# Stacks of split queries and keys through a DRAM copy, six transfers per projection, and new priorities for the order of the work

## The chip, the cores and the metric

The kernel runs on one core of a Trainium2 chip. A core has TensorE (PE, matrix products; its weight loads are shown as PEld), VectorE (DVE), ScalarE (ACT), GpSimd (POOL) and SyncE (SP, whose queue issues most DMA transfers). Each runs its own list of instructions in order and waits on semaphores for the others. The metric is the time of one execution on the device in microseconds, as the median of several runs.

## The reference

The input is `x`, 16 graphs of 1024 nodes with 256 features, and one adjacency matrix of 1024 x 1024. Four layers follow each other, each `x = x + layer(relu(layernorm(x)))`. The first three are graph attention; in short, with `H` = 4, 1 and 1 heads:

```python
q = h @ W                                   # (B, N, H*D)
e = leaky_relu(e_src[:, :, None] + e_dst[:, None, :])
attn = softmax(where(adj > 0, e, -big), over neighbours)
out = elu(attn @ q)                         # relu in the second layer
```

The fourth is a transformer block with eight heads of 32 features:

```python
q, k, v = split(h @ w_qkv)
scores = einsum('fnhd,fmhd->fhnm', q, k) / sqrt(32)
t = softmax(where(adj > 0, scores, -1e9)) @ v
y = layernorm(h + t)
out = layernorm(y + relu(y @ w1 + b1) @ w2 + b2)
```

All is float32.

## The kernel before

Everything of interest is in `direct` (a second path, `general`, runs only if a check of number ranges fails, and does not run here). A graph has eight tiles of 128 nodes (`NT = 8`), two halves of 512 nodes (`HALF`), and two groups of four heads in the fourth layer (`CT = 2`, `HG = 4`).

**Recording and planning.** No function issues instructions at once. `pe`, `act`, `dve`, `pool` and `dma` append a piece of work to a record, with its planned duration and the buffers that it writes and reads. After all 16 graphs are recorded, `schedule` (L189) orders every engine's list: it walks through a planned time, and on each engine takes, of the work that is ready, that of the lowest key. The key comes from `priority` (L136): the number of the graph plus a value on a line through knots (`KNOTS`, L283), one set for each stage (`gat0` to `gat2` for the graph attention layers, `values` and `steps` for the fourth layer's attention, `feed` for its feed-forward part, `last` for that of the last graph, `beside` for the second graph's first layer), with a shift per engine (`LEAD`). So work of several graphs is interleaved, and the knots decide how. `PASS` (L117) is the planned time in which a result reaches another engine, `SWITCH` and `BIAS` are the planned cost of TensorE's mode changes, `SLACK` and `AHEAD` belong to the model of transfers (L260 to L263). The planned times only set the order; on the chip, semaphores decide when an instruction starts.

**The graph attention layers** (`gat`, L725). Transposes (L529), projection (L770), a row of exponentials that goes to DRAM and comes back on all partitions (L843, L852), weights on VectorE (L868), then products: L895 for one head, and for four heads L982 and L992, which use the matrix engine as four column tiles of 32.

**The fourth layer's attention** (`attention`, L1082). For each group and half, `project` (L1125) makes queries or keys: a product (L1132), a copy rounded to float32r on ScalarE called `hi` (L1141), and the rest `lo = x - hi` on VectorE (L1144). There is one `hi` and one `lo` buffer. A score then is one float32r product over 128 rows in which each head's 32 features stand four times (hi.hi, hi.lo, lo.hi, lo.lo), so each head's rows of `hi` and `lo` have to be moved to a stack, `qs` for queries and `ks` for keys: 4 blocks of 32 partitions, with the four heads side by side. Sixteen transfers from on-chip memory to on-chip memory on SyncE's queue do this (L1154), each 32 partitions of 2 KB, 64 KB in all. Eight projections are made for each graph; `later` sets before which step the last five are recorded.

Then come 32 steps per graph (group, half, tile of keys): scores (L1352), exponentials on ScalarE (L1376), mask on VectorE (L1385), two steps later the product with the values and with ones (L1217, column tiles again). Some of the sums over tiles are made on VectorE (L1244) and by accumulating transfers from GpSimd's queue (L1253). At the end of each half are copies (L1292), transposes and the division. `feed` follows (L1449 and around), with the input brought back from DRAM (L1502) and the result stored (L1574). `x` is loaded at L1597 and put into DRAM at L1634.

On-chip rings set how far work can run ahead: four matrix result banks `sc` for scores and projections, four `bank`, six buffers `pa`, one `ks`, two `qs`.

Of the kernel before, what the change touches and what calls it, by code (L numbers as in the profile page):

```python
# [113 lines left out]


WEIGHT = {"pe": 1.0, "dve": 0.3}
PASS = {"pe": 0.198, "act": 0.153, "dve": 0.202, "pool": 0.13, "dma": 0.0}  # L117


class Work:  # L120


    def __init__(self, engine, us, emit, key, modes, moved, lands):
        self.engine, self.us, self.emit, self.key, self.modes = engine, us, emit, key, modes
        self.pass_on = PASS[engine]
        self.moved = moved
# [9 lines left out]
def priority(x):  # L136
    base, knots, total, lead = x.stream
    at = x.pos / max(total, 1e-9) * (len(knots) - 1)
    k = max(0, min(int(at), len(knots) - 2))
    key = base + knots[k] + (knots[k + 1] - knots[k]) * (at - k)  # L140
    return round(key - (LEAD.get(x.engine, 0.0) if lead else 0.0), 6)


class Record:
# [44 lines left out]
    def schedule(self):  # L189
        for n, x in enumerate(self.work):  # L190
            x.n = n
            if x.key is None:
                x.key = priority(x)
            x.left = len(x.before)
            for y in x.before:
                y.after.append(x)
        free = dict.fromkeys(PASS, 0.0)
        queue = 0.0
        future = {e: [] for e in PASS}
        now = {e: [] for e in PASS}  # L200
        mode = "full"
        for x in self.work:
            if not x.left:
                heapq.heappush(future[x.engine], (x.ready, x.n, x))

        def opening(x):

            at, need = 0.0, {}
            for buf in x.opens:
                need[buf.ring] = need.get(buf.ring, 0) + 1  # L210
            for ring, n in need.items():
                if len(ring.free) < n:
                    return None
                at = max(at, sorted(ring.free)[n - 1][0])
            return at

        def turn(x):

            return BIAS * SWITCH.get((mode, x.modes[0]), 0.0) if x.engine == "pe" else 0.0

        def choose(e):

            at = free[e]
            while future[e] and future[e][0][0] <= at:
                x = heapq.heappop(future[e])[2]
                heapq.heappush(now[e], (x.key, x.n, x))
            best = None
            for key, n, x in now[e]:
                t = opening(x)
                if t is not None:  # L230
                    best = min(best or (1e9,), (max(at, t), key + turn(x), n, x))
            if future[e] and (best is None or future[e][0][0] < best[0]):
                for t, n, x in sorted(future[e]):
                    if opening(x) is not None:
                        t = max(t, at, opening(x))
                        best = min(best or (1e9,), (t, x.key + turn(x), n, x))
                        break
            return best

        order = []  # L240
        while True:
            choices = [(c, e) for c, e in ((choose(e), e) for e in PASS) if c]
            if not choices:
                break
            (at, _, n, x), e = min(choices, key=lambda c: c[0][0])
            if (x.key, n, x) in now[e]:
                now[e].remove((x.key, n, x))
                heapq.heapify(now[e])
            else:
                future[e].remove((x.ready, n, x))  # L250
                heapq.heapify(future[e])
            for buf in x.opens:
                _, k = heapq.heappop(buf.ring.free)
                buf.k, buf.t = k, buf.ring.tiles[k]
            us = x.us
            if e == "pe":
                us += SWITCH.get((mode, x.modes[0]), 0.0)
                mode = x.modes[1]
            x.start = at
            if x.moved:  # L260
                queue = max(at + (us if e == "pool" else 0.2), queue) + x.moved
                us = max(us, queue - at - AHEAD)
                x.pass_on = queue + x.lands + SLACK - (at + us)  # L263
            order.append(x)
            free[e] = at + us
            for buf in x.shared:
                buf.end = max(buf.end, at + us + x.pass_on)
                buf.uses.remove(x)
                if not buf.uses:
                    heapq.heappush(buf.ring.free, (buf.end, buf.k))  # L270
            for y in x.after:
                y.ready = max(y.ready, at + us + (x.pass_on if y.before[x] else 0.0))
                y.left -= 1
                if not y.left:
                    heapq.heappush(future[y.engine], (y.ready, y.n, y))
        assert len(order) == len(self.work)
        self.end = max(free.values())
        return order


AHEAD = 3.5
SLACK = 0.56
KNOTS = {  # L283
    "gat0": (-6.706, -3.534, -2.307, -1.522, -2.815),
    "gat1": (0.005, 0.503, 0.618, 0.731, 0.916),
    "gat2": (0.938, 0.468, 0.637, 0.867, 1.15),
    "beside": (0.241, 1.203, 1.943, 0.54, 4.121),
    "values": (1.06, -3.362, -0.305, 3.145, 0.767),
    "steps": (1.014, 1.448, 1.59, 2.064, 1.794),
    "feed": (2.016, 2.165, 2.509, 2.154, 2.609),  # L290
    "last": (2.808, 3.335, 3.547, 5.206, 6.138),
}
BIAS = 1.225
LEAD = {"act": 9.55, "dve": -0.732}

SWITCH = {
    ("full", "col4"): 0.137,
# [7 lines left out]
def act_us(n, pointers=0, sbuf=0):  # L305
    return (n / 1.2 + 41 + 50 * sbuf + 101 * pointers) / 1000
# [14 lines left out]
def mm_us(n):  # L321
    return 2 * max(2 * n / 2.4 + 3.0, 109) / 1000
# [5 lines left out]
def direct(ctx, tc, flag, x, adj, gat_w, gat_a, w_qkv, ln1_g, ln1_b, ln2_g, ln2_b, w1, b1, w2, b2, out):  # L328


    nc = tc.nc
# [3 lines left out]
    HALF = N // 2  # L335
    TH = NT // 2
    D3 = C // H3
    HG = P // D3
# [31 lines left out]
    def ring(name, n, shape, pool=work):  # L370
        return Ring([pool.tile([P] + shape, F32, name=f"{name}{i}") for i in range(n)])
# [32 lines left out]
    dram = ctx.enter_context(tc.tile_pool(name="dram", bufs=1, space=DRAM))  # L404
    r_x3 = ring("x3", 3, [NT, C], dram)
    r_rd = ring("rd", 4, [P], dram)
    r_rt = ring("rt", 1, [P])
    r_sc = ring("sc", 4, [HALF], psum)
    r_bank = Shared([psum.tile([P, HALF], F32, name=f"bank{i}") for i in range(4)])
# [8 lines left out]
    def pe(us, emit, w, r, modes=("full", "full")):  # L418
        rec.add("pe", us, emit, w, r, modes)

    def act(us, emit, w, r):
        rec.add("act", us, emit, w, r)
# [7 lines left out]
    def dma(moved, lands, emit, w, r, key=None, us=0.57, engine="dma"):  # L430
        rec.add(engine, us, emit, w, r, key=key, moved=moved, lands=lands)
# [650 lines left out]
    def attention(b, xt, b_mv, b_rstd):  # L1082
# [42 lines left out]
        def project(g, hf, keys, stack, at):  # L1125

            sc, hi, lo = r_sc.new(), r_hi.new(), r_lo.new()
            c0 = keys * C + g * P

            def product():  # L1130
                for ct in range(CT):
                    nc.tensor.matmul(  # L1132
                        sc.t,
                        wqkv_sb[:, ct, c0 : c0 + P],
                        hT.t[:, ct, hf * HALF : (hf + 1) * HALF],
                        start=ct == 0,
                        stop=ct == CT - 1,
                    )

            pe(CT * mm_us(HALF), product, [sc], [b_qkv] + [hT((ct, hf)) for ct in range(CT)])  # L1140
            act(act_us(HALF), lambda: nc.scalar.copy(hi.t.bitcast(F32R), sc.t), [hi], [sc])  # L1141
            dve(
                tt_us(HALF),
                lambda: nc.vector.tensor_sub(lo.t, sc.t, hi.t),  # L1144
                [lo],
                [sc, hi],
            )
            for a in range(4):
                part = ((hi, hi, lo, lo), (hi, lo, hi, lo))[keys][a]
                for r in range(HG):  # L1150
                    dma(
                        0.3,
                        1.5,
                        lambda: nc.sync.dma_start(  # L1154
                            stack.t[a * D3 : (a + 1) * D3, r, at : at + HALF],
                            part.t[r * D3 : (r + 1) * D3, :],
                        ),
                        [stack((r, hf if keys else 0, a))],
                        [part],
                        us=0.59,  # L1160
                    )

        def values(it):
            sc = r_sc.new()
# [47 lines left out]
        steps = [(g, hf, jt) for g in range(CT) for hf in range(2) for jt in range(NT)]  # L1212
# [19 lines left out]
        for n in range(len(steps) + LAG):  # L1232
            m = n - LAG
            if m >= 0:
                g, hf, jt = steps[m]
# [12 lines left out]
                elif jt % run:  # L1248
                    for ss, pt in zip(sums[g, hf], pas[m]):
# [6 lines left out]
                            us=1.135,  # L1256
# [81 lines left out]
            if n < len(steps):  # L1338
                g, hf, jt = steps[n]
# [928 lines left out]
```

## Time and profile before

| what | value |
|---|---|
| median of 3 runs | 4092.49 us (4090.72 to 4097.2) |
| the profiled execution's own time | 4091.28 us |
| its span, first to last instruction | 4089.5 us |
| mean granted TensorE clock | 0.995 |
| busy: PE, PEld, DVE, ACT, POOL | 98%, 58%, 86%, 66%, 16% |
| mean DMA rate | 95 GB/s |
| SyncE's queue / GpSimd's queue | 22.4% / 16.2% of the 16 DMA engines' time |
| L1154, stack transfers | 2048, median 0.588 us of SyncE each |

The profile is one execution. Busy time of an engine is the union of its instructions' spans. Matmuls are pipelined and overlap, so that a busy PE is not PE at its peak. A line number is that of the kernel's source; a name such as `qs<-lo` says which tile is written from which.

### The profile page before, as it was taken

To read this page: it belongs to the slowest core of one execution; us is meant where nothing else is said; L and a number is where in the kernel's file an instruction comes from. 1 tells how busy PE (TensorE), PEld (TensorE's weight loads), DVE (VectorE), ACT (ScalarE), POOL (GpSimd) and SP (SyncE) were. 2 spreads that over 40 slices of the span, in tenths; PEclk is the share of its full clock that TensorE was granted. 3 is DMA by queue.
4 is the path that set the end of the run, shared out by engine and by line. 5 is a ranking of instruction groups with operands and counts; after the bars stand their busy time and mean duration, and the time that the engine had idled before them with its cause. 6 is when DMAs were issued, how large, how long until landed. Compare 5 with 4: busy or idle time off the path is not lost.

```text
span 4089.5 us, 68377 instructions
## 1 busy us (share of the span) xinstructions
PE 4023.3 (98%) x23874; PEld 2354.7 (58%) x23874; DVE 3499.0 (86%) x5994; ACT 2689.9 (66%) x6673; POOL 646.7 (16%) x631
## 2 busy tenths in 40 slices
PE   7999999999999999999999999999999999999998
PEld 3566466564655646566564665646556465665643
DVE  7768898988979799897988989889797998979866
ACT  5467676775757767576675767757577675765765
POOL 1102011121211202111121211212111011111100
PEclk9999999999999999999999999999999999999999
DMA  3024344343444324443243443434443244432441
GB/s 128 24 77 102 99 109 99 89 93 98 101 112 102 90 75 112 114 108 90 77 105 99 109 105 87 95 92 103 110 109 85 74 112 113 108 90 59 107 103 47
DMA packets 215248, 389.65 MB, mean 95 GB/s; under 512 B 45168, under 2 KB 80240, under 8 KB 214896
## 3 DMA queue, kind: packets, MB, share of 16 engines
q1 hardware_dynamic: 180336, 259.36, 22.4%
q0 software_dynamic: 34560, 125.84, 16.2%
q8 instruction: 191, 3.13, 0.3%
q14 instruction: 161, 1.32, 0.1%
HBM read 91.03 MB, written 33.95 MB: 31 GB/s over the span
## 4 chain that ended last, share of the span: by engine, by line
PE 85%; DVE 5%; ACT 4%; SPq 2%; DMA 2%; issue 1%; POOL 1%; DVEq 0%; ACTq 0%; POOLq 0%
PE bank L895 20%; PE bank L1217 14%; PE sc L1352 11%; PE bank L982 9%; PE bank L770 9%; PE bank L529 6%; PE bank L992 5%; PE bank L1449 4%; PE sc L1132 4%; PE sc L1169 2%; SPq L1154 2%; DVE pt L868 2%; DVE pa L1385 1%; POOL rstdz L466 1%; ACT waste L446 1%
## 5 line engine op out<-in xcount | busy, mean ns | idle before, releaser
L1385 DVE TENSOR_TENSOR pa<-pa,mask 128x1024 f32<-128x1024 f32 x1024 | 1221.4, 1218 | 72.4 <-ACT pa L1376 69.4
L1376 ACT ACTIVATE pa<-sc 128x512 f32<-128x512 f32 x2048 | 1098.3, 606 | 234.2 <-PE sc L1352 175.1
L868 DVE SCALAR_TENSOR_TENSOR pt<-row,e,mask 128x512 f32<-128x512 f32 x1472 | 1016.3, 744 | 62.2 <-DMA row<-rd 40.3
L895 PE MATMUL bank<-qb,pt 128*128 128x257 f32 x4096 | 942.0, 380 | 3.5 <-ACT fz L1533 3.5
L895 PEld LDWEIGHTS bank<-qb,pt 128*128 128x128 f32 x4096 | 771.3, 189 | 147.1 <-ACT pa L1376 12.6
L1352 PE MATMUL sc<-qs,ks 128*128 128x512 f32 x2048 | 717.7, 455 | 11.2 <-DMA qs<-lo 5.8
L1217 PE MATMUL bank<-pa,va 128*32 128x512 f32 x4096 | 504.8, 596 | 0.3 <-DVE pa L1385 0.2
L1352 PEld LDWEIGHTS sc<-qs,ks 128*128 128x128 f32 x2048 | 360.4, 189 | 212.3 <-ACT pa L1376 56.5
L1244 DVE TENSOR_TENSOR sums<-pa,pa 128x1024 f32<-128x1024 f32 x360 | 430.3, 1219 | 57.6 <-PE bank L1217 57.4
L982 PE MATMUL bank<-pt,qb 128*32 128x512 f32 x3840 | 468.7, 597 | 2.4 <-DVE pt L868 1.4
L770 PE MATMUL bank<-w_aug,hT 128*128 128x259 f32 (+1 forms) x1504 | 383.1, 393 | 0.5 <-ACT hT L764 0.5
L1253 POOL DMA_DIRECT2D sums<-pa x240 | 210.1, 878 | 930.5 <-DVE pa L1385 507.2
L770 PEld LDWEIGHTS bank<-w_aug,hT 128*128 128x128 f32 x1504 | 275.8, 191 | 121.1 <-ACT pa L1376 13.7
L923 ACT ACTIVATE ex<-bank,rec 128x256 f32<-128x256 f32 x256 | 122.1, 477 | 294.5 <-DVE rec L915 287.6
L982 PEld LDWEIGHTS bank<-pt,qb 128*32 128x32 f32 x3840 | 118.8, 109 | 275.9 <-issue 193.0
L1217 PEld LDWEIGHTS bank<-pa,va 128*32 128x32 f32 x4096 | 120.5, 109 | 263.0 <-issue 227.6
L992 PE MATMUL bank<-pt,e 128*32 128x512 f32 x1920 | 258.5, 592 | 0.0
L500 ACT ACTIVATE hn<-xh,mv,rstd 128x256 f32<-128x256 f32 x376 | 195.9, 592 | 93.0 <-DVE mv L490 89.1
L1132 PE MATMUL sc<-hTa,wqkv_sb 128*128 128x512 f32 x512 | 244.4, 600 | 0.1
L466 POOL TENSOR_TENSOR rstd<-rstd,neg_half 128x4 f32<-128x4 f32 x96 | 138.5, 1443 | 597.0 <-DVE rstd L458 588.3
L820 POOL TENSOR_TENSOR sum_e<-sum_e,e 128x12 f32<-128x12 f32 (+1 forms) x94 | 114.7, 1220 | 648.2 <-ACT e L781 648.1
L1141 ACT CAST hi<-sc 128x512 fp32r<-128x512 f32 x128 | 74.8, 585 | 196.4 <-PE sc L1132 72.8
(152 smaller groups left out, 4638.4 us busy)
## 6 DMA issues: line engine op xcount, KB each, us to landing
sums<-pa POOLq DMA_DIRECT2D x240, 512.0 KB, 6.0
row<-rd SPq DMA_DIRECT2D x184, 256.0 KB
ks<-hi SPq DMA_DIRECT2D x512, 64.0 KB
ks<-lo SPq DMA_DIRECT2D x512, 64.0 KB
qs<-hi SPq DMA_DIRECT2D x512, 64.0 KB
qs<-lo SPq DMA_DIRECT2D x512, 64.0 KB
xh<-in_x_dram SPq DMA_DIRECT2D x32, 512.0 KB
x<-xh SPq DMA_DIRECT2D x32, 512.0 KB
```

The lines of the kernel that those rows point to most:

```text
L529: nc.tensor.transpose(dst(k), src(k), ident[:shape, :shape])
L770: nc.tensor.matmul(g.t[:, : C + 3 * H], hT.t[:, ct, k * P : (k + 1) * P], w_aug[l][:, ct, :], start=ct == 0, stop=ct == CT - 1,)
L868: lambda: nc.vector.scalar_tensor_tensor(pt.t, row.t, e3[:, 2, jt // TH, h, jt % TH : jt % TH + 1], mask[:, jt, hf * HALF : (hf + 1) * HAL ...
L895: nc.tensor.matmul(g.t[:, : D + 1], pts[jt].t[:, k * P : (k + 1) * P], qb[:, jt, 0, :], start=jt == 0, stop=jt == NT - 1,)
L982: nc.tensor.matmul(g.t[u * D + d : u * D + d + D3, :], qb[:, j, h + u, d : d + D3], pts[u][j - jt].t, start=j == 0, stop=j == NT - 1,)
L992: nc.tensor.matmul(gd.t[c : c + D3, :], one(jt + k, h + u).to_broadcast([P, D3]), pts[u][k].t, start=jt == 0, stop=jt == NT - 2,)
L1132: nc.tensor.matmul(sc.t, wqkv_sb[:, ct, c0 : c0 + P], hT.t[:, ct, hf * HALF : (hf + 1) * HALF], start=ct == 0, stop=ct == CT - 1,)
L1217: nc.tensor.matmul(ac.t[r * D3 : (r + 1) * D3, :], columns(r), of_head(r), start=first, stop=last,)
L1244: lambda: nc.vector.tensor_add(ss.t, p0.t, p1.t),
L1352: nc.tensor.matmul(scs[r - r0].t, ks.t[:, r, jt * P : (jt + 1) * P].bitcast(F32R), q.t[:, r, :].bitcast(F32R), start=True, stop=True,)
L1376: lambda: nc.scalar.activation(pt.t[:, v, :], sc.t, AF.Exp, scale=1.0 / math.sqrt(D3)),
L1385: lambda: nc.vector.tensor_mul(pt.t, pt.t, mask[:, jt : jt + 1, i0 : i0 + HALF].to_broadcast([P, 2, HALF]),),
```

## The change

Two things are changed. First, `project` writes `hi` and `lo` (256 KB each) into a buffer in DRAM, of which there are three, and fills each of the stack's four blocks with one transfer from there; that takes all four heads at once, 128 rows of 2 KB. That makes two transfers to DRAM and four back, in place of sixteen. Second, the planner's constants and the knots are other ones; most stages have nine knots in place of five, and the model of a transfer that finds the queue full is a fixed duration in place of one that grows.

```diff
-PASS = {"pe": 0.198, "act": 0.153, "dve": 0.202, "pool": 0.13, "dma": 0.0}
+PASS = {"pe": 0.122, "act": 0.556, "dve": 0.232, "pool": 0.13, "dma": 0.0}
...
             if x.moved:
+                if e == "dma" and queue - at > BEHIND:
+                    us = max(us, HELD)
                 queue = max(at + (us if e == "pool" else 0.2), queue) + x.moved
-                us = max(us, queue - at - AHEAD)
                 x.pass_on = queue + x.lands + SLACK - (at + us)
...
-AHEAD = 3.5
-SLACK = 0.56
+BEHIND, HELD = 2.0, 1.35
+SLACK = 0.722
 KNOTS = {
-    "gat0": (-6.706, -3.534, -2.307, -1.522, -2.815),
+    "gat0": (-10.926, -10.742, -7.218, -4.626, -2.628, -2.099, -0.444, -3.636, -2.816),
...
-    "steps": (1.014, 1.448, 1.59, 2.064, 1.794),
-    "feed": (2.016, 2.165, 2.509, 2.154, 2.609),
+    "steps": (0.98, 1.188, 1.323, 1.512, 1.578, 1.712, 2.006, 2.02, 1.489),
+    "feed": (2.026, 2.163, 1.768, 1.658, 2.343, 1.828, 2.009, 2.223, 3.042),
...
 }
-BIAS = 1.225
-LEAD = {"act": 9.55, "dve": -0.732}
+BIAS = 2.241
+LEAD = {"act": 8.212, "dve": 0.635}
...
+    r_hl = ring("hl", 3, [2, HALF], dram)
...
+            hl = r_hl.new()
+            for k, part in enumerate((hi, lo)):
+                dma(0.65, 1.5, lambda: nc.sync.dma_start(hl.t[:, k, :], part.t), [hl(k)], [part])
             for a in range(4):
-                part = ((hi, hi, lo, lo), (hi, lo, hi, lo))[keys][a]
-                for r in range(HG):
-                    dma(
-                        0.3,
-                        1.5,
-                        lambda: nc.sync.dma_start(
-                            stack.t[a * D3 : (a + 1) * D3, r, at : at + HALF],
-                            part.t[r * D3 : (r + 1) * D3, :],
-                        ),
-                        [stack((r, hf if keys else 0, a))],
-                        [part],
-                        us=0.59,
-                    )
+                k = ((0, 0, 1, 1), (0, 1, 0, 1))[keys][a]
+                dma(
+                    1.0,
+                    1.83,
+                    lambda: nc.sync.dma_start(
+                        stack.t[a * D3 : (a + 1) * D3, :, at : at + HALF],
+                        hl.t[:, k, :].rearrange("(r d) n -> d r n", r=HG),
+                    ),
+                    [stack((r, hf if keys else 0, a)) for r in range(HG)],
+                    [hl(k)],
+                )
```

## The prediction

> **What bounds the kernel now.** I read the page's busy table first, then the busy time by stages, then the chain of waits in order of time at the end of the span, then TensorE's own waits there.
>
> ```profile
> span 4089.5 us, 68377 instructions
> PE 4023.3 (98%) x23874; PEld 2354.7 (58%) x23874; DVE 3499.0 (86%) x5994; ACT 2689.9 (66%) x6673; POOL 646.7 (16%) x631
> ```
>
> ```profile
> 0.00:250.00 250.00, 221.53 (x1413) 131.23 (x1414) 179.28 (x399) 129.50 (x359) 28.63 (x34) 0.97 0.23 75
> 1000.00:1250.00 250.00, 249.44 (x1502) 146.27 (x1498) 220.46 (x376) 169.04 (x426) 44.00 (x40) 1.00 0.40 98
> 3750.00:4000.00 250.00, 240.35 (x1271) 139.95 (x1270) 190.60 (x295) 167.61 (x396) 32.88 (x35) 0.99 0.42 99
> 4000.00:4090.00 90.00, 73.00 (x407) 30.43 (x405) 57.37 (x94) 51.08 (x118) 5.79 (x7) 0.92 0.15 40
> ```
>
> The stage lines give PE, PEld, DVE, ACT, POOL, granted clock, DMA share. In the middle PE is busy 249.4 of 250 us, VectorE 220, ScalarE 169: the matrix engine is the bound, and a few us per batch is all that waiting can cost. Start and end are looser.
>
> Busy PE is not dense PE, so I priced the matmuls by the distance between starts in the trace where they follow each other closely.
>
> ```profile
> 144.50 13.98 PE bank L895 x64
> ...
> 3939.25 3.57 PE bank L1217 x32
> 3949.25 5.29 PE bank L1217 x48
> ```
>
> 64 records of L895 in 13.98 us are 0.216 each plus the last one's tail. Thirty-two column-tiled records take 3.57 us and 48 take 5.29: 16 more cost 1.72, so four cost 0.43, and 3.57 - 8 x 0.43 = 0.13 is what leaving that mode costs. Entering it costs 0.094 (0.309 to the next start after a 0.215 us matmul). Over all kinds: 4096 x 0.216 (L895) + 11936/4 x 0.429 (L982, L992, L1217) + 2048 x 0.231 (L1352) + 1536 x about 0.220 (L770) + 1024 x 0.429 (L1132, L1449) + 512 x 0.216 (L1169) + about 2720 transposes x 0.109 = 3825 us dense. There are 397 column-tiled stretches x 0.23 = 92 us of mode changes. The span's other 173 us are 22 us before the first and after the last matmul, and 151 us in which a matmul came late. By stage, from the same starts: 44 us of lateness in the first 300 us, 38 us after 3700 us, and about 4.8 us in each batch between (period 247.6 us; dense work and mode changes 242.8).
>
> The end shows where the stack transfers matter:
>
> ```profile
> PE sc L1352 <- DMA qs<-lo: 5.8, 1, 5.8
> ```
>
> ```profile
> 3912.86 0.59 SPq L1154
> 3913.50 1.22 SPq L1154
> ...
> 3915.40 2.03 DMA ks<-lo
> ...
> 3923.99 1.97 DMA qs<-lo
> ...
> 3926.10 1.41 PE sc L1352 x2
> ```
>
> The last batch has nothing beside it, and its first scores wait 5.8 us for the stack. SyncE issues one small transfer per 0.63 us; two stacks are 32 issues, from 3903.5 to 3923.99, and the last lands 1.97 us later. This is the only long TensorE wait on a DMA; in the middle no matmul waits for one.
>
> **What the Trainium skill says.** "TensorEngine Tiling (Array Packing)", Key Properties: a change of tiling mode drains the array. The trace agrees: 0.13 + 0.094 us per stretch. "DMA: Bandwidth & Descriptors", Rules for kernel authors: coalesce, since under 64 KB a transfer is mostly overhead, and a DMA that reads what another wrote must wait for its semaphore. The trace agrees on the first (64 KB: 0.59 us issue, 2.0 us to land); no run here yet shows the second. "TensorE: Matmul & The Clock Gate", Part 1: after about 3.4 us without matmuls the clock halves. The trace agrees: half clock for 6.8 us from 3925.0, just after that 5.8 us wait, and for 3.4 us from 248.8.
>
> **The change, part by part.** The built programs hold the same instructions on PE, VectorE and ScalarE; only order and transfers differ.
>
> *Transfers.* 128 projections x 16 = 2048 issues of 0.63 us (81 us of SyncE per batch) become 128 x 6 = 768. The write to DRAM is 256 KB; the nearest row is the store of the result, issue 0.40, landing 2.15. The read is 256 KB; the nearest is the reload of x, issue 0.33, landing up to 3.14:
>
> ```profile
> 4069.63 2.15 DMA out_dram<-xr
> 4071.80 3.14 DMA xr<-x
> ```
>
> The destination's 32 partitions might keep the issue at 0.59; I take 0.33 to 0.63. One projection then needs, from hi's copy: 0.5 (copy) + 0.7 (lo on VectorE) + 0.4 + 2.15 (write) + 2 x 0.6 + 2.0 to 3.1 = 7 to 8 us; before 0.5 + 16 x 0.63 + 2.0 = 12.6. It adds a wait: the reads stand on SyncE's in-order queue until their write has landed, up to 2.2 us each time, and behind them stand row spreads for VectorE, reloads of x and stores. In the middle this is free: in the new order the shortest PE work between a projection and the first scores that use its stack is 23.4 us (before 18.4), three times the need. That is its cover; without it each us of lateness on all eight stacks costs 8 us per batch, over 100 us in the kernel. Hi and lo (one buffer each) come free after one landing instead of eight issues; ScalarE waited 47.7 us and VectorE 28.7 us on these in the whole kernel, both off the bound.
>
> At the end: in the new order two projections' transfers interleave. From hi: 0.5 + 12 issues x 0.33 to 0.63 (4 to 7.6) + two landings of 2.15 that the queue can't fill + 2.0 to 3.1 = 11 to 15.5 us, against 12.3 us of PE work between the second projection and its first scores (before 16.8 and 5.8 late). So it is 0 to 3 us late; I take 1. Gain 5 us, and with under 3.4 us of silence the half-clock stretch goes (6.8 x 1/2 = 3.4): 8 us. At the start the same two projections stand, with half clock once (1.7 us) and several waits of 1.3 to 2.9 us from 244 to 290 us; I take a gain of 6 (bounds 0 and 12).
>
> *Order.* Counted in the order: 413 column-tiled stretches, 24 per batch instead of 23: 16 x 0.23 = +3.7 us. Then, for each matmul that waits for a ScalarE or VectorE instruction which itself waits for a matmul, I took the dense PE work between those two matmuls, less the awaited instruction's duration in its row and 0.45 us for both hand-overs. Between the first batch's end and the last's start, 185 of 2346 such margins were under 0.6 us and 30 under zero; in the new order 28 of 2394 and 14. With up to fifteen instructions queued ahead on that engine counted as well, those under 0.6 us go from 643 to 287. The 4.8 us of lateness in one batch: seven gaps of 0.12 to 0.5 us make 2.1, ends of L1352 and transposes; the rest are gaps of some 0.05 us after nearly every change of kind. I take 1.8 of the 2.1 as gone and the rest as staying: (1.8 - 0.23) x 13 = 20 us.
>
> Bounds: nothing gained in the middle (+3.7), or all lateness gone (4.8 x 13 = 62, less 3). The new planner constants and knots have no cost except through this order.
>
> *Sum.* -20 - 8 - 6 = -34 us, with the middle's mode changes already in it; the three more at the ends are +0.7, so -33.3. From the profiled execution (span 4089.5, own time 4091.3, 1.8 around it): 4058.0; the median of the runs, 4092.5, is 1.2 above that execution: 4059.
>
> **Rivals.** *Hidden anyway.* The small gaps are the hand-overs themselves and stay, the new order's own tight places take what the old ones gave back: only the ends gain, 8 to 14 less 3.7: 4082 to 4088. For it: PE already at 249.4 of 250. Against: the margins.
>
> *The bound moves to SyncE's queue (slower).* Place: the reads waiting for the write's landing, with two row spreads behind them in the new order; VectorE then idles and quads come late. VectorE has 250 - 220 = 30 us spare per batch. With eight projections a batch and two waits each of 2.2 us, SyncE stands 35 us; it decides where landings take over 5 us instead of 2.15, or where rows are late by over 30/8 = 4 us each. At 1.5 us of TensorE time per batch beyond the gain: 4092 + 13 x 1.5 = 4112. Against: SyncE's issues fall by some 50 us per batch, DMA share is 0.40.
>
> *More than that.* All lateness of the middle goes: 59 in the middle, 0 to 14 at the ends: 4020 to 4034.
>
> **Chances.** Likeliest (4042 to 4078) 0.64; hidden anyway 0.20, half of it within the bound of what a measurement can tell (0.2%, 8 us); slower 0.12; more 0.04. Faster: 0.64 + 0.10 + 0.04 = 0.78; same 0.10; slower 0.12. The range leaves out the slower case, the highest of the hidden one and the better part of the last: 4036 to 4090.
>
> **What the changed profile would show.** Right: PE's dense share in a middle batch up, period 247.6 to about 246; SyncE's six transfers per projection with about 2.2 us between write and first read; TensorE's wait on the stack in the last batch under 3 us and no half clock there. Wrong: a TensorE or VectorE wait on the stack or on rows in every batch; landings of the DRAM copy over 5 us; a period of 248 or more, which would mean that the margins counted the wrong thing: lateness handed on through engines that were already behind.

## The result, and the profile after

The changed kernel takes 4071.35 us (median of 5 runs, 4067.71 to 4072.48), beside 4090.72 us (4087.59 to 4097.2) for the kernel before on the same chip: a ratio of 0.9947, 95% interval 0.9935 to 0.996, or 19.4 us less. Forecast were 4059 us and a range of 4036 to 4090. The sign and the range hold; the gain is 0.58 of the 33.3 us summed up.

First the same views as of before. The page of the kernel after, its busy table and transfers:

```profile
span 4070.3 us, 66071 instructions
PE 4012.3 (99%) x23874; PEld 2352.0 (58%) x23874; DVE 3501.7 (86%) x5994; ACT 2666.6 (66%) x6673; POOL 621.0 (15%) x631
...
DMA packets 227520, 456.54 MB, mean 112 GB/s; under 512 B 24688, under 2 KB 59760, under 8 KB 227184
...
HBM read 225.25 MB, written 101.06 MB: 80 GB/s over the span
```

TensorE does the same instructions in 19.2 us less span. Its busy time fell by 11 us only, since overlapping matmuls that wait a little also count as busy. What grew is the traffic: 389.65 MB became 456.54, and of that DRAM ("HBM") read 91 became 225 MB and written 34 became 101: a projection now sends out 0.5 MB and fetches 1 MB, where it moved 1 MB within the chip before.

Busy time by stages of the kernel after (PE, PEld, DVE, ACT, POOL, granted clock, DMA share, GB/s):

```profile
1000.00:1250.00 250.00, 250.00 (x1488) 147.41 (x1487) 221.16 (x380) 167.87 (x427) 39.90 (x40) 1.00 0.47 117
3750.00:4000.00 250.00, 242.00 (x1290) 137.09 (x1286) 190.36 (x292) 163.71 (x381) 37.54 (x33) 0.97 0.53 129
4000.00:4070.00 70.00, 51.08 (x280) 21.48 (x276) 40.29 (x78) 37.45 (x90) 6.84 (x7) 0.90 0.08 24
```

TensorE is the bound as before, the DMA share in the middle rose from 0.40 to 0.47, and the stage at 3750 us has a lower clock (0.97 against 0.99).

So I priced both traces by distances between matmul starts, as the prediction did. Dense work is the same in both (3825 us in the prediction, 3823 by the prices of the table below), and 22.2 us lie before the first and after the last matmul start; the rest of the span, mode changes and lateness together, fell from 244.0 to 224.8 us. The batches are marked by the first projection product of each graph (L1132 before, L1134 after; from 425.8 to 3649.4 us before, from 438.0 to 3651.8 after; 13 batches):

| stretch | before | after | difference | predicted |
|---|---|---|---|---|
| one middle batch | 247.97 us | 247.22 us | -0.75, x 13 = -9.8 | -20 |
| - gaps over 0.12 us in it | 2.30 us in 6.5 gaps | 1.40 us in 2.0 gaps | -0.9 | -1.8 |
| - shorter gaps in it | 2.82 us | 2.73 us | -0.1 | 0 |
| - column-tiled stretches in it | 23 | 24 | +0.23 us | +0.23 us |
| lateness and mode changes, up to the mark at 425.8 or 438.0 us | 55.8 us | 48.6 us | -7.2 | -6 |
| lateness and mode changes, after the mark at 3649.4 or 3651.8 us | 51.4 us | 49.2 us | -2.2 | -8 |
| - of these, from the last graph's first projection on (3898.7, 3883.3 us) | 35.9 us | 39.1 us | +3.2 | |

The split into longer and shorter gaps depends on how much is charged to the edges of a column-tiled stretch. Priced from the same starts with 0.094 us for entering and 0.13 us for leaving, the longer gaps are 1.65 us before and 1.13 us after; the fall of the two rows together, 1.0 us, is the same.

### The profile page after: what moved, and what is told of

The parts are those of the page before. It is cut to its first block, busy times and chain, and to the rows that moved or that the text cites. A ratio compares the mean times of both kernels' runs of the same rounds, so it can differ in the third digit from the quotient of the medians.

```text
span 4070.3 us, 66071 instructions
## 1 busy us (share of the span) xinstructions
PE 4012.3 (99%) x23874; PEld 2352.0 (58%) x23874; DVE 3501.7 (86%) x5994; ACT 2666.6 (66%) x6673; POOL 621.0 (15%) x631
## 2 busy tenths in 40 slices
DMA packets 227520, 456.54 MB, mean 112 GB/s; under 512 B 24688, under 2 KB 59760, under 8 KB 227184
## 4 chain that ended last, share of the span: by engine, by line
PE 94%; DMA 3%; ACT 1%; DVE 1%; issue 0%; SPq 0%; DVEq 0%; ACTq 0%; POOLq 0%
PE bank L897 21%; PE bank L1220 16%; PE sc L1355 12%; PE bank L984 11%; PE bank L772 9%; PE bank L531 6%; PE sc L1134 5%; PE bank L1452 5%; PE bank L994 5%; PE sc L1172 3%; DMA sums<-pa 2%; PE sc L531 1%; DVE pt L870 1%; ACT waste L448 0%; ACT pa L1379 0%
## 5 line engine op out<-in xcount | busy, mean ns | idle before, releaser
L897 PE MATMUL bank<-qb,pt 128*128 128x257 f32 x4096 | 941.0, 380 | 0.0
L897 PEld LDWEIGHTS bank<-qb,pt 128*128 128x128 f32 x4096 | 770.6, 190 | 143.6 <-issue 20.1
L1355 PE MATMUL sc<-qs,ks 128*128 128x512 f32 x2048 | 727.9, 457 | 2.6 <-DMA hl<-hi 1.1
L1220 PE MATMUL bank<-pa,va 128*32 128x512 f32 x4096 | 515.0, 597 | 0.0
L1355 PEld LDWEIGHTS sc<-qs,ks 128*128 128x128 f32 x2048 | 361.3, 189 | 237.9 <-ACT pa L1379 82.5
L984 PE MATMUL bank<-pt,qb 128*32 128x512 f32 x3840 | 461.7, 596 | 6.5 <-DVE pt L870 6.5
L772 PE MATMUL bank<-w_aug,hT 128*128 128x259 f32 (+1 forms) x1504 | 373.3, 389 | 0.0
L772 PEld LDWEIGHTS bank<-w_aug,hT 128*128 128x128 f32 x1504 | 280.3, 190 | 99.6 <-ACT qb L794 35.4
L984 PEld LDWEIGHTS bank<-pt,qb 128*32 128x32 f32 x3840 | 116.5, 110 | 294.8 <-issue 219.5
L1220 PEld LDWEIGHTS bank<-pa,va 128*32 128x32 f32 x4096 | 115.0, 109 | 250.6 <-issue 225.7
L1134 PE MATMUL sc<-hTa,wqkv_sb 128*128 128x512 f32 x512 | 240.0, 596 | 0.0
L468 POOL TENSOR_TENSOR rstd<-rstd,neg_half 128x4 f32<-128x4 f32 x96 | 169.2, 1762 | 362.1 <-DVE rstd L460 362.0
L1220 PE MATMUL bank<-sums,ones 128*32 128x512 f32 x1440 | 200.5, 600 | 3.9 <-DMA sums<-pa 3.7
```

What stands on the lines that cost most here:

```text
L772: nc.tensor.matmul(g.t[:, : C + 3 * H], hT.t[:, ct, k * P : (k + 1) * P], w_aug[l][:, ct, :], start=ct == 0, stop=ct == CT - 1,)
L897: nc.tensor.matmul(g.t[:, : D + 1], pts[jt].t[:, k * P : (k + 1) * P], qb[:, jt, 0, :], start=jt == 0, stop=jt == NT - 1,)
L984: nc.tensor.matmul(g.t[u * D + d : u * D + d + D3, :], qb[:, j, h + u, d : d + D3], pts[u][j - jt].t, start=j == 0, stop=j == NT - 1,)
L1134: nc.tensor.matmul(sc.t, wqkv_sb[:, ct, c0 : c0 + P], hT.t[:, ct, hf * HALF : (hf + 1) * HALF], start=ct == 0, stop=ct == CT - 1,)
L1220: nc.tensor.matmul(ac.t[r * D3 : (r + 1) * D3, :], columns(r), of_head(r), start=first, stop=last,)
L1355: nc.tensor.matmul(scs[r - r0].t, ks.t[:, r, jt * P : (jt + 1) * P].bitcast(F32R), q.t[:, r, :].bitcast(F32R), start=True, stop=True,)
```

## The experiments

Line numbers shift by a few between the kernels: L1352 of before is L1355 after (scores), L1217 is L1220 (products with values and with ones), L895 is L897. "Lateness" is time beyond dense work and mode changes. Ratios are to the kernel before, on the same chip.

| run | median us | ratio, 95% interval | one middle batch, us |
|---|---|---|---|
| kernel before | 4090.7 | | 247.97 |
| changed kernel | 4071.4 | 0.9947 (0.9935 to 0.996) | 247.22 |
| old_order_six | 4103.9 | 1.003 (1.0019 to 1.0041) | 248.54 |
| old_order_six_no_landing_wait | 4095.1 | 1.0007 (1.0 to 1.0013) | 248.55 |
| new_order_no_landing_wait | 4090.8 | 0.9996 (0.9988 to 1.0005) | 248.04 |
| quarter_of_the_reads | 4055.4 | 0.991 (0.9896 to 0.9923) | 246.30 |
| ones_product_later | 4066.6 | 0.9937 (0.9924 to 0.9951) | 246.6 |
| ones_product_two_later | 4068.3 | 0.9944 (0.9931 to 0.9958) | 246.68 |
| new_order_little_allowance | 4228.5 | 1.0335 (1.032 to 1.0351) | 257.2 |
| old_knots_more_allowance | 4300.4 | 1.0506 (1.049 to 1.0522) | 261.0 |
| new_order_sixteen | 4525.8 | 1.1065 (1.105 to 1.108) | 277.1 |
| ones_later_sixteen | 4529.0 | 1.1066 (1.1051 to 1.1081) | 277.4 |
| new_knots_sixteen_planned | 4287.7 | 1.0475 (1.0457 to 1.0492) | 262.2 |
| old_knots_six_planned | 4297.6 | 1.0497 (1.0479 to 1.0514) | 260.5 |

### The six transfers in the old order: old_order_six

```diff
             for a in range(4):
                 for r in range(HG):
-                    nc.sync.dma_start(stack block a, head r <- part, rows of head r)
+                    # r == 0, first block that uses this part: part -> hl, in DRAM
+                    # r == HG - 1: stack block a, all heads <- hl
```

> The kernel before with its order kept on TensorE, VectorE, ScalarE and GpSimd, instruction by instruction; only the sixteen transfers per projection are replaced by the six through DRAM, at the same places of SyncE's queue. Theory (the transfers matter at the two ends only, the order makes the middle): a batch in the middle takes 247.7 to 248.2 us as before (247.97), TensorE's 5.8 us wait for the stack in the last batch falls under 2 us, time 4080 to 4088. Rival (shorter use of SyncE and of the hi and lo buffers loosens every batch): a batch takes about 247.2, time about 4072 to 4077. Second rival (an order planned for another queue meets waits for the write's landing): slower than before, 4094 or more.

Measured: slower than before by 0.3%, some 12 us. A middle batch is 0.57 us longer (7.4 us in all), mostly at one place: about 50 us into a batch, at the column-tiled products of L982 (L984 here) and the L1449 kind behind them, TensorE was 0.36 us late per batch and is now 0.97 us late. It waits there for VectorE's weights `pt`, and VectorE waits for its rows. In the middle (430 to 3640 us; total, times, longest), TensorE and then VectorE, of the kernel before:

```profile
PE bank L982 <- DVE pt L868: 0.5, 1, 0.5
```

```profile
DVE pt L868 <- DMA row<-rd: 34.7, 36, 2.0
```

and of this run:

```profile
PE bank L984 <- DVE pt L870: 3.1, 7, 0.6
```

```profile
DVE pt L870 <- DMA row<-rd: 52.7, 26, 4.1
```

The rows go out no later than before (SyncE issues the first of them 38.7 to 40.7 us into a batch, before 40.2 to 41.1 us), but now two reads of 256 KB, held back until their write had landed, go out right ahead of them. That these make the rows land later fits the next run: there the reads go out 4 to 5 us earlier, and this wait is gone. At the end the last batch's first scores wait longer than before. SyncE's own waits and one wait of TensorE in this run:

```profile
SPq L1158 <- DMA hl<-lo: 519.6, 128, 6.5
...
SPq L1158 <- DMA hl<-hi: 322.7, 118, 5.8
```

```profile
PE sc L1364 <- DMA hl<-hi: 11.4, 1, 11.4
```

SyncE stands for 842 us at its reads until a write has landed, and the single long stack wait at the end went from 5.8 to 11.4 us. SyncE's queue there shows why (start, duration, what; counts of issues at the end):

```profile
3913.59 0.32 SPq L1156 DMA_DIRECT2D hl<-hi  x1
3919.11 0.33 SPq L1158 DMA_DIRECT2D ks<-hl  x1
3919.50 0.42 SPq L1156 DMA_DIRECT2D hl<-lo  x1
3923.43 1.83 SPq L1158 DMA_DIRECT2D ks<-hl  x3
```

From the write's issue to the read behind it pass 5.5 us for `hi` and 3.9 for `lo`, one after the other on the in-order queue. So the transfers by themselves lose, and the part of my forecast that put a gain at the end down to them falls. The time is what the second rival said (waits for the write's landing, 4094 or more).

### Without the wait for the landing: old_order_six_no_landing_wait, new_order_no_landing_wait

```diff
+            old = the DRAM buffer of the projection before
-                    stack block a <- hl
+                    stack block a <- old
```

> As old_order_six, but the four reads take the DRAM buffer of the projection before, which landed long ago, so that they do not wait for this projection's write; bytes, transfers and order are the same (the stacks then hold another projection's values: what is left out is that the right data are read). Theory (SyncE's standing for the write's landing made old_order_six slower, through spreads of rows and the single hi and lo buffers): back to 4086 to 4094, a batch at about 248. Rival (the added DRAM traffic slows the other transfers): stays at 4100 to 4106.

> The changed kernel with the same edit: the reads take the DRAM buffer of the projection before (its values are not the right ones) and do not wait for this projection's write. Theory (in the new order the wait is covered): within 4 us of the changed kernel, 4067 to 4074. Rival (the wait costs in the new order too): 4055 to 4064.

In the old order the time falls between the two ranges, 4095.1 us: lateness from the last graph's first projection on falls from 32.3 to 21.2 us, while a middle batch keeps its 248.55 us. That isn't the same lateness, though. The late place of old_order_six is gone, and TensorE waits at another one, for accumulating transfers about 164 us into a batch, in each of the 13. In the middle:

```profile
PE bank L1230 <- DMA sums<-pa: 8.5, 9, 1.9
```

```profile
DVE pt L870 <- DMA row<-rd: 11.8, 19, 1.3
```

So the wait for the landing costs some 11 us at the end, and in the middle taking it away exchanges one loss for another of the same size. Both runs carry the added DRAM traffic, in place of transfers within the chip; that it makes both losses is likely, but not shown. In the new order the run is some 20 us slower than the changed kernel (0.9996 and 0.9947), which neither theory nor rival had. In the middle (430 to 3640 us) TensorE's longest wait in total is this one; first of the changed kernel, then of the run without the wait:

```profile
PE bank L1220 <- DMA sums<-pa: 3.2, 6, 1.5
```

```profile
PE bank L1222 <- DMA sums<-pa: 9.0, 9, 1.7
```

Those are the accumulating transfers from GpSimd's queue, for which the product with ones waits. A tenth of them took over 7.33 us from issue to landing in the changed kernel, over some 7.9 without the wait; the longest took 9.77 and 10.36. VectorE's wait for rows hardly differs here (24.2 and 22.6 us), so the landing's wait is covered in the new order. A reading of the slowdown that fits, only argued: without the wait the reads start beside the writes and crowd the accumulating transfers more, and the queue's wait spaced them.

### A quarter of the reads: quarter_of_the_reads

```diff
+                R = HG if b == 0 else 1
-                        stack.t[a * D3 : (a + 1) * D3, :, at : at + HALF],
-                        hl.t[:, k, :].rearrange("(r d) n -> d r n", r=HG),
+                        stack.t[a * D3 : (a + 1) * D3, :R, at : at + HALF],
+                        hl.t[: R * D3, k, :].rearrange("(r d) n -> d r n", r=R),
```

> The changed kernel in which, from the second graph on, each read brings one head of four (64 KB in place of 256 KB; the other three heads keep the first graph's values, so three quarters of the stack's refilling is left out). Order and waits are the same. Theory (the accumulating transfers that TensorE waits for are late because they share the DMA engines with the reads): that wait shrinks, 4064 to 4068. Rival (they are late by their own place in the order): 4069 to 4073.

Some 15 us less than the changed kernel by the ratios (0.991 and 0.9947), 20.0 by the spans of the profiled executions, and so below both ranges: the theory had the direction. A middle batch is 0.92 us shorter (12.0 in all), and from the last graph's first projection on 8.1 us are gone (lateness 32.2 to 24.1). TensorE has no wait for an accumulating transfer in the middle any more; their median fell from 5.98 to 5.40 us. This prices the reads, not the bytes that the change added: in the kernel before, with the sixteen small transfers, the same median was 5.96 us, and a tenth took over 7.33 us, as in the changed kernel. TensorE waits for these transfers after the change also because the new order puts a product where less work stands before it. Over the whole run the group of products with ones went from

```profile
L1220 PE MATMUL bank<-sums,ones 128*32 128x512 f32 x1440 | 200.5, 600 | 3.9 <-DMA sums<-pa 3.7
```

to this (busy, mean ns | idle before it, and what ended it):

```profile
L1221 PE MATMUL bank<-sums,ones 128*32 128x512 f32 x1440 | 191.5, 600 | 0.5 <-DMA sums<-pa 0.5
```

3.4 us less idle and 9 us less busy for the same 1440 products: most of such a wait stands in the busy time of overlapping records, and only the distances between starts show it. Together that is 12.4 us, about as much as the 13 middle batches are shorter by.

### The waiting product one instruction later: ones_product_later, ones_product_two_later

The trace shows one such wait as a chain. Of the changed kernel, the chain of work in order of time (start, duration, what), and TensorE around it:

```profile
1290.48 0.47 ACT ex L925
1290.96 1.47 ACT pa L1379 x3
1292.42 0.42 issue
1292.84 7.82 DMA sums<-pa
1300.66 0.04 issue
1300.71 1.91 PE bank L1220 x12
```

```profile
1299.42 1.03 PE L1220 MATMUL bank<-sums,ones 128*32 128x512 f32 x4
1300.71 0.62 PE L1220 MATMUL bank<-sums,ones 128*32 128x512 f32 x2 [0.26 <-DMA sums<-pa]
```

The transfer took 7.82 us where 6.0 is the median, and for that long TensorE had only so much work before the product (0.26 us shown as idle; 1.29 us from start to start, 0.86 beyond the dense 0.43 of four). Such a wait stands 121 to 123 us after a batch's mark in 8 of the 13.

```diff
+                    if run == 4 and jt == 3 and g == 0:
+                        late.append(rec.work[-1])
...
+        for x in late:                       # two_later: for x in late + late
+            i = order.index(x)
+            j = next(k for k in range(i + 1, len(order)) if order[k].engine == "pe")
+            if not any(x in y.before for y in order[i + 1 : j + 1]):
+                order.insert(j, order.pop(i))
```

> The changed kernel with one product per group of heads (the product with ones after the fourth tile of the second half) put behind the next piece of TensorE's work; all else stays in its place. In the changed kernel that product waits 0.6 to 2.1 us for an accumulating transfer in 8 of 13 middle batches. Theory (that wait is time lost, and the product put behind it is ready): up to 0.86 us gained in each of these batches, 4 to 8 us in all: 4064 to 4067. Rival (the time is given back at the next wait): within 2 us of the changed kernel, 4070 to 4073.

> As ones_product_later, but the product with ones goes behind two pieces of TensorE's work, the second being scores: 13 more column-tiled stretches, 13 x 0.23 = 3 us, against the 0.3 us per batch of this wait that ones_product_later has left, 4 us. Theory: no further gain, 4064 to 4068, and no wait of TensorE for an accumulating transfer in the middle. Rival (the wait had pushed other work as well): 4061 or less.

`g == 0` makes it one product per graph, that of the first group of heads, not one per group as the first expectation says. One instruction later gives 4066.6 us, where the changed kernel has 4071.4. The intervals of the two ratios overlap, so these intervals don't prove it; the traces say where the gain is: gaps over 0.12 us fall from 1.40 to 0.75 us per batch, the batch from 247.22 to 246.6, and the wait is gone from the middle's list. One instruction more brings nothing further, as expected. ones_product_later computes the whole result and has the lowest median of all that do.

### The planner's constants: new_order_little_allowance, old_knots_more_allowance

```diff
-PASS = {"pe": 0.122, "act": 0.556, ...}     # changed kernel
+PASS = {"pe": 0.122, "act": 0.153, ...}
-PASS = {"pe": 0.198, "act": 0.153, ...}     # kernel before
+PASS = {"pe": 0.198, "act": 0.556, ...}
```

> The changed kernel with one planner constant put back: the allowance for ScalarE's results from 0.556 to 0.153 us. The work is the same; the order has 516 column-tiled stretches instead of 413, and margins under zero are 70 instead of 14 (378 instead of 21 when fifteen queued instructions are counted). Theory (lateness follows those margins): 103 stretches x 0.23 = 24 us, and 2 or more us of further lateness per batch: 4105 to 4140. Rival (the margins say nothing, only stretches count): 4071 + 24 = 4095, a batch's lateness staying at 4.1 us.

> The kernel before with one constant changed: the allowance for ScalarE's results from 0.153 to 0.556 us, knots and sixteen transfers as before. 501 column-tiled stretches instead of 397; margins under zero 69 instead of 30 (260 instead of 99 with fifteen queued instructions). Theory (lateness follows the margins of the order that comes out, not the constant): 104 x 0.23 = 24 us and about 1 us more lateness per batch: 4115 to 4135. Rival (a larger allowance is what made the changed kernel faster): lateness per batch falls from 5.1 to about 4, and the time is 4091 + 24 - 14 = 4101 or less.

The first had the direction, at two to five times the size (157 us above the changed kernel, where 34 to 69 were expected); the second was far off: more allowance for ScalarE's results, given to the old knots, costs 13 us per batch. The constant isn't good or bad by itself. Margins below zero, with fifteen instructions queued ahead counted, were 99 for before, 21 after, 378 and 260 in these two; lateness per batch was 5.1, 4.1, about 12 and about 16 us. The count separates tight orders from the two good ones, but ranks the last two the wrong way round and gives no size.

### Sixteen transfers in the new order: new_order_sixteen, ones_later_sixteen

```diff
-                dma(0.65, 1.5, lambda: nc.sync.dma_start(hl.t[:, k, :], part.t), [hl(k)], [part])
+                dma(0.65, 1.5, lambda: None, [hl(k)], [part])
...
-                    lambda: nc.sync.dma_start(stack block a, all heads <- hl.t)
+                    four transfers: stack block a, head r <- (hi, lo)[k], rows of head r
```

> The changed kernel's own order on TensorE, VectorE, ScalarE and GpSimd, with the sixteen small transfers back on SyncE's queue at the places of the four reads (the two writes are left out, nothing goes through DRAM); the result is the whole one. This is the fourth corner of order by transfers: old order with sixteen 4091, old with six 4104, new with six 4071. Theory, that the DRAM copy's traffic costs 0.9 us a batch in the new order too and about 8 us at the end: a middle batch of 246.3 us as with a quarter of the reads, so -12; at the end the 32 issues of 0.6 us of two projections, 20 us, stand against 12.3 us of TensorE work, so 8 to 10 us late, about as much as the six cost there: together 4055 to 4065. Rival, that the new order leaves SyncE too little room for 81 us of issues a batch (rows and stores behind them come late, hi and lo come free after eight issues in place of one landing): a middle batch of 248 or more, 4080 to 4105, with VectorE waits on rows over 50 us in the whole kernel.

> Both: sixteen small transfers in the new order, and the fourth tile's ones-product one TensorE instruction later. Theory: once the DRAM traffic is gone the accumulating transfers land in time, so the move of the ones-product brings nothing more: within 2 us of new_order_sixteen, 4055 to 4065. Rival: the two gains are different things and add, 5 us below new_order_sixteen.

Theory and rival both fell, by over 400 us. The run doesn't compute the whole result either, as I had put it: in this order 47 of the 128 projections have `hi` or `lo` refilled by the next projection before all their blocks are fetched (126 of 512 blocks), and such a block gets the next projection's rows. With one `hi` and one `lo` this order of the work can't be had without the copy. It isn't fast either. Of VectorE's waits in this run (total, times, longest):

```profile
DVE lo L1146 <- DMA ks<-lo: 180.9, 31, 7.3
...
DVE lo L1146 <- DMA qs<-lo: 109.3, 14, 18.9
...
DVE lo L1146 <- DMA ks<-hi: 63.4, 11, 6.4
```

VectorE stands 354 us at the head of its queue because `lo` is held by eight issues in place of one landing; TensorE then waits 147.5 us for `lo` at its scores and 53.0 at the values' product, and a batch takes 277.1 us. The changed kernel's VectorE waits 8.0 us in all for `lo` to come free (its write's landing), ScalarE 73.7 us for `hi`. Whether the product's place would matter without the traffic isn't told by the second run: other waits cover it.

### Each half alone, planned for: new_knots_sixteen_planned, old_knots_six_planned

The first is the changed kernel with the sixteen transfers of before declared to the planner; the second is the kernel before with the six transfers as the change declares them. Each gets an order of its own and computes the whole result.

> One half of the change alone: the new constants and knots, with the sixteen on-chip transfers of before, declared to the planner as before (it makes an order of its own; the result is the whole one). That order has 491 column-tiled stretches in place of 397 (94 x 0.23 = +22 us) and 267 margins below zero with fifteen instructions queued (before 99, after 21, new_order_little_allowance 378 for some 12 us of lateness a batch, old_knots_more_allowance 260 for some 16). Theory, that the gain of the change is one order which the new constants give only together with the six transfers: 5 to 11 us a batch more and the stretches, 4170 to 4260. Rival, that the new knots are better whatever the transfers: 4100 or less.

> The other half alone: the six transfers through DRAM, declared to the planner as in the changed kernel, with the constants and knots of before (an order of its own; the result is the whole one). 482 column-tiled stretches (+20 us) and 512 margins below zero with fifteen queued, more than in any run so far. Theory: 10 us a batch or more and the stretches, 4220 to 4350. Rival, that fewer and larger transfers help where the planner knows of them: 4100 or less.

Direction as the theory had it in both; the first is 28 us beyond its range: lateness of about 18 us per batch in both, where 9 to 16 and over 15 were expected. So the four corners, knots by transfers, each planned for itself, are 4091 (old, sixteen), 4288 (new, sixteen), 4298 (old, six) and 4071 (new, six). The parts don't add: each alone costs 5%, both together save 0.5%. But one planner constant changed alone cost as much above (157 and 208 us). So the four corners show that the knots fit one set of planned durations; that the transfers and the new knots suit each other in a way of their own isn't shown.

## Why the prediction was right in sign and range, and wrong in size

**Sign and mechanism: the order.** The prediction put three fifths of its gain on the order and none of the middle's on the transfers. With the same six transfers, the old order takes 4103.9 and the new one 4071.4 us, 32 us by the order alone. The transfers alone cost some 12. The three terms of the profiled executions, -9.8 - 7.2 - 2.2 = -19.2 us, make up the difference of the spans.

**The middle, -20 predicted and -9.8 measured.** The failed step is "I take 1.8 of the 2.1 as gone". The old long gaps did go, as the margins said: of the 2.30 us per batch that they made before, 0.04 are left at the same places. Put at nothing was what would come in their place, and 1.40 us did. Most of it is of a kind that the margins didn't count: they looked at ScalarE and VectorE instructions only, and here TensorE waits for a transfer, the accumulating one, at one place of the new order (0.91 us per batch), besides a gap once per batch between L1355 and L772 (0.24 to 0.45 us by the price taken for the score before it). Two runs show it: moving the product by one instruction takes 0.65 us per batch off the long gaps; with a quarter of the reads the wait is gone too, and the batch is 0.92 us shorter. (The lateness of a batch before, taken as 4.8 us, is 5.1 by these marks.)

**The cover of the transfers in the middle.** "In the middle this is free" holds for what it counted: no scores of the middle wait for a stack, and in the new order VectorE's wait for rows in the middle is no longer than before (24.2 us in all, before 34.7). It looked at SyncE's queue and at the 23.4 us before the first scores, not at who else uses the DMA engines. In the old order the six transfers cost 0.57 us per batch, at the rows, and the same amount at the accumulating transfers where the landing isn't waited for; in the new order TensorE's wait for an accumulating transfer goes when three quarters of the reads do (0.92 us per batch). The page "DMA: Bandwidth & Descriptors" of the Trainium skill, Rules for kernel authors, states that transfers from SyncE, ScalarE and GpSimd all run on the same 16 engines and interleave; the landings of `sums<-pa` above agree (median 5.98 us, 5.40 with a quarter of the reads). The same section's advice to coalesce, which the prediction cited, doesn't decide here: old_order_six follows it and loses, with 67 MB more to move and reads that wait for a landing.

**The landing.** The nearest row was 2.15 us for the store of the result, taken in a quiet stage. From write to first read the changed kernel shows about 3 us at 1190 us, on SyncE's queue:

```profile
1190.55 0.32 SPq L1152 DMA_DIRECT2D hl<-hi  x1
...
1193.53 0.81 SPq L1158 DMA_DIRECT2D ks<-hl  x2
...
1196.59 0.34 SPq L1152 DMA_DIRECT2D hl<-lo  x1
1199.95 0.78 SPq L1158 DMA_DIRECT2D qs<-hl  x2
```

3.0 and 3.4 us, up to 7.3 in SyncE's longest wait of that kind. In old_order_six, where a read stands directly behind a write on the queue (230 times), 4.0 us pass between the two issues at the median. The issues were as bounded (medians 0.34 to 0.43 us).

**The end, -8 predicted and -2.2 measured.** From the last graph's first projection on nothing was gained at all (+3.2 us). The stack's wait fell from 5.8 to 0.6 us, where 1 was taken, but by luck. The reading before it was slightly off too: the 5.8 us wait of before ended with the 29th of the 32 issues, not with the last. For the changed kernel 11 to 15.5 us were taken from `hi`'s copy to the stack. From the copy for the queries (3890.2 us) to the landing (3911.2 us) passed 21 us: SyncE had two stores of the result and two reloads of `x` ahead of the reads, and the second reload went out when a store had landed. Then the last read took 7.9 us to land, where 2.0 to 3.1 were taken. From the chain of work in order of time:

```profile
3897.99 3.47 DMA out_dram<-xr
...
3901.47 0.32 SPq L1505
...
3903.26 7.90 DMA qs<-hl
...
3911.20 2.08 PE sc L1355 x4
```

The wait for it is short because TensorE already stood for other things. Its waits from 3870 to 3960 us:

```profile
PE bank L531 <- ACT xh L502: 4.9, 1, 4.9
PE sc L1172 <- DVE lo L1146: 2.4, 1, 2.4
PE sc L1355 <- DMA qs<-hl: 0.6, 1, 0.6
```

The 4.9 us for ScalarE's `xh` come from the same queue. ScalarE waited for VectorE's `mv`, and VectorE stood just before it for the reload:

```profile
3906.30 0.69 DVE L1511 TENSOR_TENSOR xr<-xr,row_c 128x512 f32<-128x512 f32 x1 [4.79 <-DMA xr<-x]
```

The prediction named reloads and stores as standing on SyncE's queue, but gave them no time at the end. With a quarter of the reads VectorE waits 2.5 us there and TensorE 1.2 us for `xh`, and the end is 8.1 us shorter.

"With under 3.4 us of silence the half-clock stretch goes" failed as well: half clock is granted for 13.7 us there (3.4 from 3899.4 and 10.2 from 3906.2 us), where before had 10.2 in two places. Nor do the traces bear out 3.4 us as a limit, as the prediction read them. The longest distance between two matmul starts shortly before the half clock at 248.8 us of before is 1.8 us, before that at 4000.1 us 2.2 us, and before that at 3899.4 us of the changed kernel 2.8 us.

**The start, -6 predicted and -7.2 measured.** The size is in part luck. The half-clock stretch at 248.8 us is gone, but half clock up to the marks at 425.8 and 438.0 us is 17.1 us in both kernels: other stretches, before 50 us, are longer. Of the 7.2 us, 4.4 lie between the first projections of the first two graphs, where the prediction looked, and 2.8 before them, where it didn't; what made them less late I haven't tested.

**The rivals.** "Hidden anyway" was half right: new tight places took back half of the middle. "The bound moves to SyncE's queue" didn't come in the new order. In the old one its place was right: SyncE stood 842 us at its reads, VectorE's rows came late behind them, and the stack at the end. Not listed at all was that each part alone, planned for itself, loses 5%. "Hi and lo come free after one landing instead of eight issues" was costed at nothing, from waits of 47.7 and 28.7 us off the bound. The new order rests on that early release: the same order with sixteen transfers takes 454 us more, and stacks get the next projection's rows. What the three buffers in DRAM add to it, by letting a projection run before the stack is free, wasn't tested.

## What to carry to other kernels

Count as a margin every instruction that the bound engine waits for, transfers of other queues included, and price an added transfer also by what its bytes do to those. A change of data path and a new order are to be judged together where the order is planned around the path: here each half alone lost 5% while both won. A wait that came out as forecast may be short only because the engine stood for something else first; look at what stands beside it. When the bound engine waits at one fixed place per batch, try that one instruction one place later; here it brought some 4 us more.

## What the runs showed of the hardware that I had not expected

An accumulating transfer of 512 KB from GpSimd's queue takes 4.45 to 9.8 us to land in the changed kernel, and leaving out three quarters of the reads on SyncE's queue moves its median by 0.6 us. In the new order, taking a wait away from SyncE's queue made the kernel some 20 us slower, with later landings of those transfers. Four reads of 256 KB issued one behind the other took up to 7.9 us to land at the end. From a store to DRAM to the read behind it pass 4.0 us at the median from issue to issue in old_order_six (2.0 to 7.8), where a quiet store landed in 2.15. TensorE's clock was halved after distances between matmul starts of no more than 1.8, 2.2 and 2.8 us.
